# A fused four-layer network on one core: the third stage takes layer 3's mean from layer 2's integers, makes one transpose for both scales, and runs in a new order

## The chip, the cores and the metric

The kernel runs on one core of a Trainium2 chip. The metric is the device time of one launch in microseconds (us), as a median over runs. A core has five engines with queues of their own: TensorE (PE in the profile; its weight loads are PEld), VectorE (DVE), ScalarE (ACT), GpSimd (POOL) and SyncE (SP, which here only issues DMAs).

## What is computed

The input `x` has 8192 samples of 8 channels by 16 by 16, in float32. Four layers follow one another; each adds to `x` a function of its group-normalized self.

```python
def _gn(v, G=4, eps=1e-5):            # mean and variance of each sample over 2 channels x 16 x 16
    ...
    return ((g - m) / jnp.sqrt(s + eps)).reshape(v.shape)

x = x + _L0_conv_ref(_gn(x), core0, core1, core2, bias)   # a tensor-train operator
x = x + _L1_conv_ref(_gn(x), lin_w, lin_b, gamma, beta)   # 3x3 convolution, batch norm over all samples, relu
x = x + _L2_conv_ref(_gn(x), w2, b2)                      # 3x3 convolution of integers, see below
x = x + _L3_conv_ref(_gn(x), w3, b3)                      # 3x3 convolution with signs as weights, edge padding
```

Layer 2 quantizes: `sx = 127 / max|x|` over the whole normalized input of all samples, `qx = clip(round(x * sx), -127, 127)`, the weights likewise with `sw`, then an integer convolution divided by `sx * sw`, plus a bias for each channel. Layer 3 uses the signs of its weights times one mean for each output channel, pads by repeating the edge, and adds a bias.

## The kernel before, in words

The samples are cut into `NT = 64` tiles of 128 samples. A tile is `[128 partitions = 8 channels x 16 rows, 2048 = 128 samples x 16 columns]`, 1 MB. There are three stages over all 64 tiles, because the batch norm of layer 1 and the maximum of layer 2 need all samples.

*Stage 1* (to about 2620 us) does layers 0 and 1; its constants are made in `late_constants`, step by step between its tiles. *Stage 2* (to about 3063 us) applies the batch norm, takes the group means and deviations of layer 2's input (`stats2`, `sigma2`, kept for every tile in `gnst`), subtracts the mean (`centre2`), and takes the maximum of the absolute value per sample (`range2`); every fourth tile `range2` multiplies four tiles' maxima `top` by the reciprocal deviations `gr` and reduces them to one column of `amax`. Between the stages stand a reduction of `amax` to `pm`, an all-reduce over partitions to `gm`, and `sx` and `inv = 1/(sx*sw)`.

*Stage 3* (from about 3066 us) does layers 2 and 3. For each tile `i`:

- `rows2` (VectorE) multiplies one group scale by a mask into a diagonal (`diag_d`) and transposes it (`rows_d`); `spread2` (TensorE) multiplies that by `sel0`, so that `r2`, in the PSUM bank `ps_a`, holds the scale for every channel row and sample. `v` scales `x` to int8 (VectorE), `q` casts to bf16 (ScalarE), `bias` adds layer 2's bias to the first half of `x` (ScalarE).
- `c2h0` and `c2h1` (TensorE) are layer 2's convolution for the two halves of the samples, six bf16 matmuls each into the PSUM tile `pq`. `stz` (VectorE) adds the first half to `x`. For the second half `z1` (ScalarE) copies `pq` out with scale and bias and `add1` (GpSimd) adds it.
- `sq` squares the new `x` (ScalarE). `sums` (`sums_pe`, TensorE) sums `x` and its square over the rows of a group: for each of the two sources, four float32 matmuls with 32 output columns, one for each quarter of the samples, into the PSUM tile `s`. `small` (`stats_small`, VectorE) reduces `s` over the 16 columns, transposes the result into `ps_a` and makes mean and variance, `pow` (GpSimd) the reciprocal deviation.
- `rows3` makes a second diagonal of three parts (`diag_e`: mean times reciprocal deviation, reciprocal deviation, layer 2's mean) and transposes it; `spread3` makes `r3` (bank `ps_r`) and `o3` (bank `ps_o`). `c` copies `o3` with layer 3's bias (ScalarE).
- `t` scales `x` by `r3` (VectorE); `hi` and `lo` split it into two fp32r parts (ScalarE, GpSimd), `edl` and the end of `hi` copy the edges (ScalarE); `corr` adds `c` to `x` (GpSimd). `c3h0a`, `c3h0b`, `c3h1a`, `c3h1b` (TensorE) are layer 3's convolution: the letter says high or low part, the digit the half; six matmuls each into the PSUM tile `pf`, which shares two buffers of two banks with `pq`. `out0` and `out1` (VectorE) add the halves to `x`, and the tile is stored.

The order of stage 3 on every engine is written out by hand: operation `op` of tile `i` is due at `PERIOD * i + PHASE[op]`, and `todo` is the sorted list of these. The due times order the instructions only; each engine then runs its own list in this order and waits by semaphore for what it needs. `InOrder` fixes that order, and since it records every operation in its own line, nearly all instructions show as L43. The tiles `u`, `xs`, `ys`, `bs`, `xk` in profile rows are the slots in which `x` lives.

Of the kernel before, what the change touches and what calls it, by code (L numbers as in the profile page):

```python
# [8 lines left out]
F32 = mybir.dt.float32  # L9
# [4 lines left out]
ALU = mybir.AluOpType  # L14
# [18 lines left out]
class InOrder:  # L33
# [5 lines left out]
    def __getattr__(self, name):  # L39
        op = getattr(self.engine, name)  # L40

        def call(*args, **kwargs):
# [5 lines left out]
PERIOD = 11.539  # L48
PHASE = {"rows2": 0, "spread2": 0.01, "v": 5.1, "q": 10.2, "bias": 10.4, "c2h1": 11.6, "z1": 13.1, "c2h0": 16.1, "add1": 17.1,
         "stz": 23.1, "sq": 24, "sums": 31.8, "small": 34.7, "pow": 37.3, "rows3": 42.7, "spread3": 45.3, "t": 46.3,  # L50
         "hi": 49.9, "c": 51.2, "lo": 51.9, "corr": 58.8, "edl": 60.3, "c3h0a": 60.4, "c3h0b": 61.3, "out0": 66.8,
         "c3h1a": 69.3, "c3h1b": 69.4, "out1": 69.41}

# [4 lines left out]
PACK2 = [("w2all", C * C * 9), ("w3all", C * C * 9)]  # L58
# [3 lines left out]
def tile_net(ctx: ExitStack, tc: tile.TileContext, xb, xt_in, pack0, pack1, pack2, out):  # L62
# [35 lines left out]
    LATE = 5 if NT >= KEEP + STAY + 3 else 0  # L98

# [47 lines left out]
    def late_constants(late):  # L147
# [37 lines left out]
        L["grp"] = grp = blocks(32, 1.0 / 512, "grp")  # L185
        b1 = L["b1"] = const.tile([P, 1], F32, name="b1")
# [65 lines left out]
        dve.tensor_copy(gpad[:, :, 0:G], quarter.unsqueeze(1).to_broadcast([P, NQ, G]))  # L252
        for k, name in enumerate(("sel0", "sel1", "corr")):

            t = L[name] = const.tile([P, CH], F32, name=name)
            dve.tensor_copy(t.rearrange("p (g n) -> p g n", g=G),
                            mod32[:, G * k:G * k + G].unsqueeze(2).to_broadcast([P, G, CH // G]))
# [12 lines left out]
    amax = const.tile([P, NT // 4], F32, name="amax")  # L270
# [4 lines left out]
    def samples(t):  # L275
        return t.rearrange("p (b w) -> p b w", w=W)
# [425 lines left out]
    def stats_small(mv, st, ps, name):  # L702

        s = small.tile([P, 32], F32, name=f"s_{name}", tag="s")
        dve.tensor_reduce(s, samples(ps), AX.X, ALU.add)
        dve.transpose(st, s)
        sq = small.tile([P, G], F32, name=f"sq_{name}", tag="sqm")
        dve.tensor_copy(mv[:, 0:G], st[:, 0:G])
        dve.tensor_tensor(sq, st[:, 0:G], mv[:, 0:G], ALU.mult)
        dve.scalar_tensor_tensor(mv[:, G:2 * G], st[:, G:2 * G], EPS, sq, ALU.add, ALU.subtract)  # L710

# [20 lines left out]
    with tc.tile_pool(name="p2", bufs=2) as p2, tc.tile_pool(name="ps2", bufs=2, space=PSUM) as ps2:  # L732
# [16 lines left out]

        def sum2(i):  # L750
            x, y = T[i]["x"], T[i].pop("y")
            y_used[i] = y
            act.activation(y, y, AF.Relu, bias=bn_b, scale=bn_a)
            pool.tensor_tensor(x, x, y, ALU.add)
# [9 lines left out]
        def stats2(i):  # L764

            st, mv = psc[:, 32 + 32 * (i % 2):64 + 32 * (i % 2)], gnst[:, order2[i]]
            red = small.tile([P, 32], F32, name=f"s_c{i}", tag="s")
            dve.tensor_reduce(red, samples(T[i].pop("ps")), AX.X, ALU.add)
            dve.transpose(st, red)
            T[i]["sq"] = small.tile([P, G], F32, name=f"sq_c{i}", tag="sqm")  # L770
            act.copy(mv[:, 0:G], st[:, 0:G])
            act.activation(T[i]["sq"], st[:, 0:G], AF.Square)

        def sigma2(i):
            st, mv = psc[:, 32 + 32 * (i % 2):64 + 32 * (i % 2)], gnst[:, order2[i]]
            dve.scalar_tensor_tensor(mv[:, G:2 * G], st[:, G:2 * G], EPS, T[i].pop("sq"), ALU.add, ALU.subtract)
            stats_pow(mv)

        def spread2(i):
            T[i]["gb"] = ps = ps2.tile([P, BANK], F32, name=f"gb_{i}", tag="gb")  # L780
            rows = to_rows(diag[i % 2], mask2, [gnst[:, order2[i]]], f"c{i}")
            if i % 4 == 0:
                T[i]["gr"] = ps2.tile([P, 4, P], F32, name=f"gr_{i}", tag="gr")
                T[i]["top"] = p2.tile([P, 4, P], F32, name=f"top_{i}", tag="top")
            else:
                T[i]["gr"], T[i]["top"] = T[i - 1]["gr"], T[i - 1]["top"]
            for dst, sel in ((ps[:, 0:P], L["sel0"]), (T[i]["gr"][:, i % 4], L["sel1"])):
                pe.matmul(dst, sel, rows, start=True, stop=True)
# [16 lines left out]
        def range2(i):  # L805

            top = T[i]["top"]
            for a, b in HALVES:
                dve.tensor_reduce(top[:, i % 4, a:b], samples(T[i]["x"])[:, a:b], AX.X, ALU.max,
                                  apply_absolute_value=True)  # L810
            if i % 4 == 3:
                dve.tensor_tensor(top, top, T[i]["gr"], ALU.mult)
                dve.tensor_reduce(amax[:, i // 4:i // 4 + 1], top.rearrange("p a b -> p (a b)"), AX.X, ALU.max)

        def on(i, f):
            if 0 <= i < NT:
                f(i)
# [10 lines left out]
        for i in range(NT + 4):  # L828
            if i == 1:
                on(free, load2)  # L830
            if i + AHEAD2 < NT - LATE:
                on(i + AHEAD2, lambda i: i <= free or load2(i))
            elif late:
                k, j = late.pop(0)
                T2[j][k] = y_used[i - 1]
                nc.sync.dma_start(T2[j][k], (x1_d if k == "x" else y_d)[order2[j]])
            on(i, sum2)
            on(i - 2, sums2)
            on(i - 3, spread2)
            on(i - 1, square2)  # L840
            on(i - 2, stats2)
            on(i - 3, centre2)
            on(i - 2, sigma2)
            on(i - 3, range2)
# [4 lines left out]
    gm = const.tile([P, 1], F32, name="gm")  # L849
    nc.vector.tensor_reduce(pm, amax, AX.X, ALU.max)  # L850
# [3 lines left out]
    nc.vector.tensor_tensor(inv, sx, L["sw"], ALU.mult)  # L854
    nc.vector.reciprocal(inv, inv)

    gv = gnst[:, :, G:2 * G]
    nc.vector.tensor_scalar(gv, gv, sx, None, ALU.mult)
# [4 lines left out]
    with ExitStack() as s:  # L863
        wk = s.enter_context(tc.tile_pool(name="wk3", bufs=2))
        ps_c = s.enter_context(tc.tile_pool(name="ps_c3", bufs=2, space=PSUM))
        ps_s = s.enter_context(tc.tile_pool(name="ps_s3", bufs=1, space=PSUM))
        order = [*kept, *(t for t in range(NT) if t not in kept)]

        sq3, t3, z3 = sqs[0], [sqs[1], xh], [y_stay[3][:, h * F // 2:(h + 1) * F // 2] for h in range(2)]
        T = [dict() for _ in range(NT)]  # L870
        AHEAD = min(NT, KEEP - 6)
        diag2, diag3 = diagonal("d"), diagonal("e")
# [4 lines left out]
        mask, st3 = ps_a[:, P:P + NQ], ps_a[:, P + 32:P + 64]  # L877
# [12 lines left out]
        def rows2(i):  # L890
            T[i]["rows2"] = to_rows(diag2[i % 2], mask, [gnst[:, order[i], G:2 * G]], f"d{i}")

        def rows3(i):
            mv = T[i].pop("mv")
            mr = small.tile([P, G], F32, name=f"mr_{i}", tag="mr")
            dve.tensor_tensor(mr, st3[:, 0:G], mv[:, G:2 * G], ALU.mult)
            T[i]["rows3"] = to_rows(diag3[i % 2], mask, [mr, mv[:, G:2 * G], gnst[:, order[i], 0:G]], f"e{i}")


        def spread2(i):  # L900
            pe.matmul(r2, L["sel0"], T[i].pop("rows2"), start=True, stop=True)

        def spread3(i):
            rows = T[i].pop("rows3")
            pe.matmul(r3, L["sel1"], rows, start=True, stop=True)
            pe.matmul(o3, L["corr"], rows, start=True, stop=True)
# [14 lines left out]
        def bias2(i):  # L921
            x = halves(T[i]["x"])[:, 0]
            act.activation(x, x, AF.Identity, bias=L["bias2"], scale=1.0)
# [13 lines left out]

        def second2(i):
            act.activation(z3[i % 2], T[i].pop(("pq", 1)), AF.Identity, bias=L["bias2"], scale=inv)

        def add2(i):
            x = halves(T[i]["x"])[:, 1]
            pool.tensor_tensor(x, x, z3[i % 2], ALU.add)
# [4 lines left out]
        def sums3(i):  # L948
            T[i]["ps"] = ps_s.tile([P, BANK], F32, name=f"s3_{i}", tag="s3")
            sums_pe(T[i]["ps"], T[i]["x"], sq3)  # L950

        def stats3(i):
            T[i]["mv"] = small.tile([P, 2 * G], F32, name=f"mv3_{i}", tag="mv")
            stats_small(T[i]["mv"], st3, T[i].pop("ps"), f"d{i}")

        def pow3(i):
            stats_pow(T[i]["mv"])
# [44 lines left out]
        def finish(i, h):  # L1002
# [4 lines left out]
            if T[i]["done"] == 2:  # L1007
# [3 lines left out]
        OPS = {"rows2": rows2, "spread2": spread2, "v": scale2, "q": round2, "bias": bias2,  # L1011
               "c2h0": lambda i: layer2(i, 0), "stz": first2, "c2h1": lambda i: layer2(i, 1), "z1": second2, "add1": add2,
               "sq": square3, "sums": sums3, "small": stats3, "pow": pow3, "rows3": rows3, "spread3": spread3, "c": offset3,
# [3 lines left out]
        todo = [(op, i) for _, op, i in sorted((PERIOD * i + at, op, i) for op, at in PHASE.items() for i in range(NT))]  # L1017
        for i in range(AHEAD):
            load3(i)
        for op, i in todo:  # L1020
            if op == "rows2" and AHEAD <= i + 4 < NT:
                load3(i + 4)
            OPS[op](i)

# [68 lines left out]
```

## Time and profile before

| | |
|---|---|
| median of 3 runs | 3824.15 us (3823.85 to 3824.85) |
| profiled execution, own time / span | 3824.58 / 3822.8 us |
| busy over the span | PE 94%, DVE 89%, POOL 80%, ACT 66% |
| stage 1, 0 to 2620 us | PE busy 2601.65, DVE 2311.57 |
| stage 2, 2620 to 3062 us | DVE busy 395.72, DMA share 0.94 |
| stage 3, 3062 to 3823 us | PE busy 738.24, POOL 721.85, DVE 678.72, ACT 583.94 |

Busy shares are of the span, so an engine may be full in one stage and idle in another. A profile row gives a group of instructions as `out<-in`, the shape, the count, and the mean time of one in nanoseconds; durations overlap where instructions are pipelined, so that the step from one start to the next start is what an engine pays in a full queue.

### The profile page before, as it was taken

The numbers are of one execution on the slowest core, as the hardware profiler recorded it, in microseconds if no ns is written. First come the engines' busy times: TensorE is split into PE (matmuls) and PEld (weight loads), VectorE is DVE, ScalarE is ACT, GpSimd is POOL, SyncE is SP. The second block draws the span as 40 slices with busy tenths as digits, with TensorE's granted clock in tenths as the row PEclk, the third lists the DMA queues.
The fourth block names the chain that finished last, engine by engine and source line by source line (L and its number), as shares of the span: only waits on it lengthen the run. The fifth ranks groups of instructions, "written<-read, shape, count | busy, mean of one in ns | idle before, by whom it ended". The sixth has DMA issues, their size and how long they took to land.

```text
span 3822.8 us, 52777 instructions
## 1 busy us (share of the span) xinstructions
PE 3598.8 (94%) x16264; PEld 2127.1 (56%) x16326; DVE 3386.0 (89%) x6313; ACT 2518.2 (66%) x2676; POOL 3048.8 (80%) x3104
## 2 busy tenths in 40 slices
PE   8999999999999999999999999997665589999999
PEld 4666666666666666666666666663221145555555
DVE  8988888888888888888888888877998889999997
ACT  5666666666666666666666666665665578778775
POOL 4877777778777777787777777865887779999998
PEclk9999999999999999999999999998776689999999
DMA  5787787878877878878788878766999724444442
GB/s 212 254 270 256 258 269 252 265 258 258 271 253 261 272 253 262 262 250 272 254 263 270 257 258 265 253 200 253 419 424 424 326 90 186 182 183 187 181 161 110
DMA packets 210809, 960.93 MB, mean 251 GB/s; under 512 B 44896, under 2 KB 45152, under 8 KB 110048
## 3 DMA queue, kind: packets, MB, share of 16 engines
q1 hardware_dynamic: 173808, 692.22, 48.8%
q0 software_dynamic: 36288, 264.26, 23.5%
q8 instruction: 131, 2.15, 0.2%
q14 instruction: 150, 1.23, 0.1%
q10 hardware_dynamic: 432, 1.08, 0.1%
HBM read 578.84 MB, written 378.54 MB: 250 GB/s over the span
## 4 chain that ended last, share of the span: by engine, by line
PE 85%; DVE 6%; DMA 4%; issue 2%; POOL 1%; ACT 1%; POOLq 0%; SPq 0%; DVEq 0%; ACTq 0%
PE po L43 45%; PE pu L43 12%; PE pf L43 10%; PE pm L43 6%; PE pq L43 4%; PE s L43 3%; PE pc L43 3%; DVE top L43 3%; PE ps_r L43 1%; DMA ys<-x_d 1%; DMA x_d<-u 1%; DMA x_d<-ys 1%; DMA u<-x_d 1%; DMA x_d<-xs 1%; DMA sq<-y_d 1%
## 5 line engine op out<-in xcount | busy, mean ns | idle before, releaser
L43 PE MATMUL po<-u,core 128*128 128x512 f32 (+1 forms) x4112 | 1844.7, 591 | 0.0
L43 ACT COPY u<-pu 128x2048 f32<-128x2048 f32 x512 | 955.4, 1866 | 512.9 <-PE pu L43 512.8
L43 PEld LDWEIGHTS po<-u,core 128*128 128x128 f32 x4112 | 744.6, 190 | 737.0 <-issue 736.1
L43 PE MATMUL pu<-core2r,xl 128*128 128x256 f32 x4032 | 678.6, 310 | 4.5 <-ACT u L43 3.5
L43 PEld LDWEIGHTS pu<-core2r,xl 128*128 128x128 f32 x4032 | 527.9, 189 | 127.9 <-issue 123.1
L43 POOL TENSOR_TENSOR bs<-bs,xh 128x512 fp32r<-128x512 f32 (+1 forms) x253 | 325.1, 1285 | 203.0 <-ACT xh L43 203.0
L43 POOL TENSOR_TENSOR v<-e 128x128 f32<-128x128 f32 x750 | 396.7, 540 | 0.0
L43 DVE TENSOR_TENSOR xs<-po,xs 128x512 f32<-128x512 f32 x256 | 176.9, 691 | 218.8 <-PE po L43 218.6
L43 ACT ACTIVATE m<-pm,b 128x128 f32<-128x128 f32 x250 | 91.7, 367 | 395.3 <-PE pm L43 395.3
L43 PEld LDWEIGHTS pm<-v,fast 128*128 128x128 f32 x2000 | 262.5, 192 | 119.7 <-issue 105.7
L43 POOL TENSOR_TENSOR e<-x1n,x 128x512 f32<-128x512 f32 x250 | 305.9, 1223 | 23.2 <-ACT x L43 15.8
L43 DVE TENSOR_TENSOR bs<-bs,stat 128x1024 f32<-128x1024 f32 x252 | 290.6, 1215 | 2.1
L43 POOL TENSOR_TENSOR xs<-xs,w 128x2048 f32<-128x2048 f32 x64 | 291.4, 4552 | 0.6 <-DMA xs<-in_xt 0.6
L43 PE MATMUL pm<-v,fast 128*128 128x128 f32 x2000 | 263.6, 275 | 0.0
L43 ACT ACTIVATE x<-x1n 128x512 f32<-128x512 f32 x500 | 247.0, 545 | 7.6 <-DVE x1n L43 7.6
L43 POOL TENSOR_TENSOR mv<-mv,mhalf 128x4 f32<-128x4 f32 x127 | 130.8, 1030 | 135.9 <-DVE mv L43 135.9
L43 PE MATMUL pf<-hi,sign 128*128 128x512 f32 x768 | 231.1, 439 | 0.0
L43 POOL DMA_DIRECT2D xl<-limb_d x252 | 149.8, 594 | 101.3 <-ACT x L43 38.4
L43 PE MATMUL pf<-lo,sign 128*128 128x512 f32 x768 | 218.0, 422 | 0.3 <-ACT lo L43 0.3
L43 POOL TENSOR_TENSOR v<-r 128x128 f32<-128x128 f32 x500 | 215.2, 447 | 0.0
L43 ACT ACTIVATE sq<-xs 128x2048 f32<-128x2048 f32 x103 | 197.0, 1913 | 18.2 <-DVE xs L43 13.6
L43 PE MATMUL gb<-rows_c,sel 128*128 128x128 f32 x128 | 40.8, 413 | 166.3 <-DVE rows_c L43 166.3
(308 smaller groups left out, 7195.3 us busy)
## 6 DMA issues: line engine op xcount, KB each, us to landing
xl<-limb_d POOLq DMA_DIRECT2D x252, 1024.0 KB, 7.4
x_d<-xs SPq DMA_DIRECT2D x76, 1024.0 KB, 8.4
xs<-in_xt SPq DMA_DIRECT2D x64, 1024.0 KB, 7.6
bs<-in_xb SPq DMA_DIRECT2D x63, 1024.0 KB, 5.6
limb_d<-xh SPq DMA_DIRECT2D x1008, 64.0 KB, 4.4
limb_d<-bs SPq DMA_DIRECT2D x1008, 64.0 KB, 5.2
y_d<-ys SPq DMA_DIRECT2D x60, 1024.0 KB, 8.0
u<-x_d SPq DMA_DIRECT2D x34, 1024.0 KB, 6.5
```

Of the source, the lines that this page charges most:

```text
L43: return self.tc.keep_in_program_order(op(*args, **kwargs))
```

## The change

It touches three places.

In the setup the bias of layer 2 gets its group mean taken off, which moves to layer 3's bias. A small job at tile 8 of stage 2 (`operands3`) makes bf16 weights `total` that sum layer 2's convolution over output rows, and a selection matrix `back2`.

In stage 3 `sums` no longer multiplies `x`: it multiplies the integers `q` by `total` (high and low part of the weights, three column taps each, four quarters: 24 bf16 matmuls, of which eight cover 512 columns and sixteen 32). `cols` holds, for each tile, four columns of group values side by side: layer 3's two, layer 2's mean, and layer 2's scale of the tile `LEAD = 4` later. So one product, one transpose and three matmuls (`rows`, `spread`) serve both scales, and the separate `rows2` and `spread2` go. The squared mean (`sqm`) is ScalarE's, the variance (`var`) stays on VectorE. Of the second half of layer 2, `SHARE = 16` samples (256 of 1024 columns) go to VectorE (`stz1`); `bias` covers them. The table of due times is new.

At the end of stage 2 `range2` finishes tiles 60 to 62 with tile 62 and tile 63 by itself, and `inv` is made later, after the first scaling.

```diff
-PERIOD = 11.539
-PHASE = {"rows2": 0, "spread2": 0.01, "v": 5.1, "q": 10.2, "bias": 10.4, "c2h1": 11.6, "z1": 13.1, "c2h0": 16.1, "add1": 17.1,
-         "stz": 23.1, "sq": 24, "sums": 31.8, "small": 34.7, "pow": 37.3, "rows3": 42.7, "spread3": 45.3, "t": 46.3,
-         "hi": 49.9, "c": 51.2, "lo": 51.9, "corr": 58.8, "edl": 60.3, "c3h0a": 60.4, "c3h0b": 61.3, "out0": 66.8,
-         "c3h1a": 69.3, "c3h1b": 69.4, "out1": 69.41}
+PERIOD = 10.966
+PHASE = {"v": 0, "q": 3.7, "c2h1": 10.5, "bias": 10.6, "stz1": 12.1, "z1": 12.9, "c2h0": 14, "stz": 15.2, "add1": 17.2,
+         "sq": 20.8, "sums": 21.9, "small": 23.5, "sqm": 25.4, "var": 26.5, "pow": 30.4, "rows": 32.9, "spread": 33.3,
+         "c": 35, "t": 41.2, "hi": 43.2, "lo": 49, "edl": 52.9, "corr": 55.8, "c3h1a": 61.3, "c3h1b": 61.5, "c3h0a": 62.1,
+         "c3h0b": 62.4, "out1": 65, "out0": 65.8}
+LEAD = 4
+SHARE = 16
...
+        pair = w["bias2all"].rearrange("p (g k) -> p g k", k=C // G)
+        dve.tensor_tensor(pair, pair, grp.unsqueeze(2).to_broadcast([P, G, C // G]), ALU.mult)
+        mb = const.tile([P, 1], F32, name="mb")
+        dve.tensor_reduce(mb, w["bias2all"], AX.X, ALU.add)
+        dve.tensor_scalar(mb, mb, 512.0 * G / C, None, ALU.mult)
+        dve.tensor_tensor(L["bias2"], L["bias2"], mb, ALU.subtract)
+        dve.tensor_tensor(L["bias3"], L["bias3"], mb, ALU.add)
...
+        def operands3():
+            part = const.tile([P, 3, G], F32, name="part")
+            total = L["total"] = const.tile([P, 6, 32], BF16, name="total")
+            dve.memset(total, 0.0)
+            dve.tensor_reduce(part.rearrange("p k g -> p (k g)"), L["band2"].rearrange("p k (g n) -> p (k g) n", g=G), AX.X, ALU.add)
+            for k in range(0, 3, 2):
+                dve.tensor_tensor(part[:, 1], part[:, 1], part[:, k], ALU.add)
+                dve.tensor_scalar(part[:, k], part[:, k], -1.0, None, ALU.mult)
+            dve.tensor_copy(total[:, 0:3, 0:G], part)
+            dve.tensor_tensor(total[:, 3:6, 0:G], part, total[:, 0:3, 0:G], ALU.subtract)
+            L["select"]("back2", [3], L["band3"][:, 0])
...
-            if i % 4 == 3:
-                dve.tensor_tensor(top, top, T[i]["gr"], ALU.mult)
-                dve.tensor_reduce(amax[:, i // 4:i // 4 + 1], top.rearrange("p a b -> p (a b)"), AX.X, ALU.max)
+            if i % 4 == 3 or i == NT - 2:
+                a, b, at = (3, 4, i // 4) if i == NT - 1 else (0, i % 4 + 1, NT // 4 if i == NT - 2 else i // 4)
+                dve.tensor_tensor(top[:, a:b], top[:, a:b], T[i]["gr"][:, a:b], ALU.mult)
+                dve.tensor_reduce(amax[:, at:at + 1], top[:, a:b].rearrange("p a b -> p (a b)"), AX.X, ALU.max)
...
+    cols = wk.tile([P, NT + LEAD, 4 * G], F32, name="cols", bufs=1)
+    nc.vector.memset(cols[:, 0:LEAD, 0:3 * G], 0.0)
+    nc.vector.memset(cols[:, NT:, 3 * G:4 * G], 0.0)
+    nc.scalar.copy(cols[:, LEAD:, 2 * G:3 * G], gnst[:, :, 0:G])
...
-    nc.vector.tensor_tensor(inv, sx, L["sw"], ALU.mult)
-    nc.vector.reciprocal(inv, inv)
-
-    gv = gnst[:, :, G:2 * G]
-    nc.vector.tensor_scalar(gv, gv, sx, None, ALU.mult)
+    nc.vector.tensor_scalar(cols[:, 0:NT, 3 * G:4 * G], gnst[:, :, G:2 * G], sx, None, ALU.mult)
...
+        def column(i, k):
+            return cols[:, i + LEAD, k * G:(k + 1) * G]
 
         def rows3(i):
-            mv = T[i].pop("mv")
-            mr = small.tile([P, G], F32, name=f"mr_{i}", tag="mr")
-            dve.tensor_tensor(mr, st3[:, 0:G], mv[:, G:2 * G], ALU.mult)
-            T[i]["rows3"] = to_rows(diag3[i % 2], mask, [mr, mv[:, G:2 * G], gnst[:, order[i], 0:G]], f"e{i}")
+            if i >= 0:
+                dve.scalar_tensor_tensor(column(i, 0), st3[:, 0:G], inv512, column(i, 1), ALU.mult, ALU.mult)
+            diag = diag3[i % 2]
+            dve.tensor_tensor(diag[:, :, 0:4 * G], cols[:, i + LEAD].unsqueeze(1).to_broadcast([P, NQ, 4 * G]),
+                              mask.unsqueeze(2).to_broadcast([P, NQ, 4 * G]), ALU.mult)
+            T3[i] = rows = small.tile([P, P], F32, name=f"rows_{i}", tag="rows")
+            dve.transpose(rows, diag.rearrange("p q j -> p (q j)"))
 
         def spread3(i):
-            rows = T[i].pop("rows3")
-            pe.matmul(r3, L["sel1"], rows, start=True, stop=True)
-            pe.matmul(o3, L["corr"], rows, start=True, stop=True)
+            rows = T3.pop(i)
+            for k, (dst, sel) in enumerate(((r2, "back2"), (r3, "sel1"), (o3, "corr"))):
+                if (i >= 0 if k else i + LEAD < NT):
+                    pe.matmul(dst, L[sel], rows, start=True, stop=True)
...
         def bias2(i):
-            x = halves(T[i]["x"])[:, 0]
+            x = T[i]["x"][:, 0:F // 2 + SHARE * W]
...
+        def third2(i):
+            x = halves(T[i]["x"])[:, 1][:, 0:SHARE * W]
+            dve.scalar_tensor_tensor(x, T[i]["pq", 1][:, 0:SHARE * W], inv, x, ALU.mult, ALU.add)
+
         def second2(i):
-            act.activation(z3[i % 2], T[i].pop(("pq", 1)), AF.Identity, bias=L["bias2"], scale=inv)
+            act.activation(z3[i % 2][:, SHARE * W:], T[i].pop(("pq", 1))[:, SHARE * W:], AF.Identity, bias=L["bias2"], scale=inv)
 
         def add2(i):
-            x = halves(T[i]["x"])[:, 1]
-            pool.tensor_tensor(x, x, z3[i % 2], ALU.add)
+            x = halves(T[i]["x"])[:, 1][:, SHARE * W:]
+            pool.tensor_tensor(x, x, z3[i % 2][:, SHARE * W:], ALU.add)
...
         def sums3(i):
             T[i]["ps"] = ps_s.tile([P, BANK], F32, name=f"s3_{i}", tag="s3")
-            sums_pe(T[i]["ps"], T[i]["x"], sq3)
+            ps, qs = T[i]["ps"], samples(T[i]["q"])
+            for j in range(2):
+                for k, w in ((1, slice(0, W)), (0, slice(W - 1, W)), (2, slice(0, 1))):
+                    for q in range(NQ):
+                        pe.matmul(samples(ps)[32 * q:32 * q + 32, :, w], L["total"][:, 3 * j + k],
+                                  qs[:, q * QS:(q + 1) * QS, w], start=(j == 0 and k == 1), stop=False)
+            for q in range(NQ):
+                pe.matmul(ps[32 * q:32 * q + 32], L["wsum"][:, 1], sq3[:, q * BANK:(q + 1) * BANK], start=False, stop=True)
 
         def stats3(i):
-            T[i]["mv"] = small.tile([P, 2 * G], F32, name=f"mv3_{i}", tag="mv")
-            stats_small(T[i]["mv"], st3, T[i].pop("ps"), f"d{i}")
+            red = small.tile([P, 32], F32, name=f"s_{i}", tag="s")
+            dve.tensor_reduce(red, samples(T[i].pop("ps")), AX.X, ALU.add)
+            dve.transpose(st3, red)
+
+        def square_mean3(i):
+            T[i]["sqm"] = small.tile([P, G], F32, name=f"sqm_{i}", tag="sqm")
+            act.activation(T[i]["sqm"], st3[:, 0:G], AF.Square, scale=inv512)
+
+        def variance3(i):
+            dve.scalar_tensor_tensor(column(i, 1), st3[:, G:2 * G], EPS, T[i].pop("sqm"), ALU.add, ALU.subtract)
...
         for op, i in todo:
-            if op == "rows2" and AHEAD <= i + 4 < NT:
+            if not ready and op not in ("rows", "spread", "v"):
+                ready = True
+                dve.tensor_tensor(inv, sx, L["sw"], ALU.mult)
+                dve.reciprocal(inv, inv)
+                dve.tensor_scalar(inv512, inv, 1.0 / 512, None, ALU.mult)
+            if op == "v" and AHEAD <= i + 4 < NT:
                 load3(i + 4)
             OPS[op](i)
...
```

## The prediction

> **What bounds it now.** Start with the page's chain of waits, then ask which stage the change is in.
>
> ```profile
> PE 85%; DVE 6%; DMA 4%; issue 2%; POOL 1%; ACT 1%; POOLq 0%; SPq 0%; DVEq 0%; ACTq 0%
> ```
>
> TensorE carries most of the chain. The change lies mainly in the third stage (3066 to 3818 us), so read busy time by stretches of ten tiles there (after the span: PE, PEld, DVE, ACT, POOL, clock, DMA share, GB/s):
>
> ```profile
> 3223.00:3337.70 114.70, 114.17 (x571) 67.52 (x580) 105.43 (x191) 91.32 (x81) 113.64 (x41) 1.00 0.49 186
> 3337.70:3452.40 114.70, 114.18 (x572) 67.52 (x580) 105.43 (x191) 91.29 (x81) 112.81 (x41) 1.00 0.47 181
> ```
>
> Both PE and POOL look full, which busy time alone can't settle. The chain inside one tile does:
>
> ```profile
> 3231.30 1.85 PE s L43 x16
> 3233.15 0.42 PE ps_r L43 x2
> 3233.57 0.22 PE ps_o L43 x2
> 3233.79 0.22 PE ps_a L43 x2
> 3234.02 1.30 PE pq L43 x6
> 3235.31 6.15 PE pf L43 x24
> 3241.46 0.66 PE pq L43 x3
> 3242.12 0.05 issue
> 3242.18 0.59 PE pq L43 x2
> 3242.77 1.85 PE s L43 x16
> ```
>
> These pieces sum to the 11.47 us from one `s` to the next; no other engine appears. So the tile period is TensorE's own sum, 11.47, and POOL stands just below: per tile lo 4.28, corr 3.69, add1 2.42, pow 1.02 = 11.41 by the groups. A microsecond taken off POOL, DVE or ACT is worth nothing alone; one off `s` is worth 64.
>
> Inside `s`, TensorE's timeline for one tile:
>
> ```profile
> 3426.27 1.07 PE L43 MATMUL s<-bs,wsum 128*32 128x512 f32 x8
> 3427.16 1.04 PE L43 MATMUL s<-sq,wsum 128*32 128x512 f32 x8
> 3428.13 0.49 PE L43 MATMUL ps_r<-rows_e,sel 128*128 128x128 f32 x2
> ```
>
> Start to start, the x half takes 0.89 and the square half 0.97. Single records explain it: four matmuls, one for each group of 32 output columns, start 7 ns apart and run together, in two fp32 passes 0.43 apart.
>
> **What the skill says.** "TensorE: Matmul & The Clock Gate", Part 3, says that matmuls on different column groups run concurrently: the 7 ns agree. Its "Wait — 56ns, not 53.3ns?" gives a floor of 25 ns between matmuls however small, and 62 ns each where the sequencer decodes them in software: no small bf16 matmul runs in this trace, so these become upper prices below. "PSUM — Partial Sum Buffer", "PSUM bank collisions raise a hardware error", has ScalarE and VectorE kept off one bank even as two readers. The trace agrees: late in stage 2 VectorE subtracts one half of `gb` and needs nothing from ScalarE, yet waits for ScalarE's copy `gm` of the other half of that bank. From the waits (total, times, longest, us):
>
> ```profile
> DVE yk L43 <- ACT gm L43: 0.8, 2, 0.4
> ```
>
> **Part 1: the mean from layer 2's integers.** Removed: the x half, 0.88 (single records). Added: for each of two bf16 weight parts, a full 512-column set of four concurrent matmuls and two edge sets of 32 columns: 24 matmuls, 24 weight loads. A full bf16 set of 512 columns is paced at 0.216 (pq's pace), so two cost 0.43. Four edge sets: lower bound 4 × 0.02 (28 ns of starts at 7 ns); upper, four starts at the skill's 25 ns, 0.10 each. I take 0.045, since each weight load must precede its matmuls and cannot hide behind so short a set. With 0.03 for the first load: 0.43 + 0.18 + 0.03 = **0.64**, between 0.52 and 0.88. The switch to column groups (pq's last start to `s` is 0.31 instead of 0.216) stays. Gain 0.24 per tile, 15.6 us over 64; bounds 0 and 23. The layer-2 integers are read later, so ScalarE's q of two tiles on must wait for them (two buffers). Behind q on ScalarE stand edl and sq; but q also waits for v, which ends later than those sums do, so this wait should not bind.
>
> **Part 2: one diagonal and transpose.** VectorE loses diag_d 0.16, rows_d 0.31, two of three diag_e 0.33, the mv copy 0.16 and sq_d 0.16: 1.12 busy. The remaining diagonal grows to 64 elements, +0.05; the product mr becomes one instruction of like cost. ScalarE gains the squared mean, about 0.18 (stage 2's sq_c row). PE still runs three spread matmuls a tile. var now waits for that squared mean, with t and out1 behind it on VectorE; stz stands between small and var, 1.2 us in which ScalarE has 0.2 us to do. v's scale now comes from the spread of the tile four before, so v waits for nothing new: VectorE's order is v, rows, and only then can PE overwrite r2. Worth nothing by itself: PE covers it.
>
> **Part 3: a quarter of the second half moves.** 256 of 1024 columns leave add1 (2.42 → 1.81 POOL), go to VectorE (1242 ns for 1024 scales to about 0.44), and make bias 1.15 → 1.36 and z1 1.19 → 0.98 on ScalarE. POOL's sum becomes 10.81. This matters: had POOL stayed at 11.41, it would have kept nearly all of part 1.
>
> **Part 4: the new order.** A fixed order on four engines runs at its longest loop: an engine's own sum, or a chain that returns to its start one period later. Take both. TensorE: 11.47 - 0.24 = **11.23**. POOL 10.81. VectorE, start to start: before 11.47 - 0.62 idle (waiting on pf) = 10.85; less about 0.75 and plus 0.36 (issue-spaced), 10.5. ScalarE about 9.7 (hi and its edges 2.45, sq 1.91, q 1.90, bias 1.36, z1 0.98, edl 0.55, c 0.36, squared mean 0.2). The new wait is z1 behind stz1 (same bank). Its loop: layer-2 half 0 ends, 0.2, stz 1.17, var 0.15, t 2.29, out1 1.19, v 2.26, rows 0.68, out0 1.16, stz1 0.51, z1 1.03, matmul start 0.1 = 10.75. z1 releases the bank pair for layer 3's first half; behind it on ScalarE stand c, squared mean and q. 10.75 < 11.23, so TensorE stays the bound with POOL 0.4 behind; whatever the sums cost, no more can be had than 11.47 → 10.8.
>
> **Part 5: from the last range to the first scaling.** On VectorE now:
>
> ```profile
> 3055.84 0.18 DVE L43 TENSOR_TENSOR diag_b<-gnst,mask 128x32 f32<-128x32 f32 x1
> ...
> 3059.59 2.34 DVE L43 TENSOR_REDUCE top<-sq 128x64 f32<-128x1024 f32 x2
> 3059.70 0.32 SPq L803 DMA_DIRECT2D x_d<-sq  x1
> 3062.03 0.69 DVE L43 TENSOR_TENSOR top<-top,gr 128x512 f32<-128x512 f32 x1
> 3062.76 0.69 DVE L43 TENSOR_REDUCE amax<-top 128x1 f32<-128x512 f32 x1
> ```
>
> The last pair shrinks from 512 to 128 elements: about -0.8. But tile 62's new pair over 384 (2 × 0.6) comes ahead of tile 63's diagonal in VectorE's program order, hence on the same path: +1.2. inv and its reciprocal leave: -0.1 to -0.2; two small memsets and a wider diagonal, +0.2. Net +0.4 (-0.8 to +0.8): this way isn't shorter. inv's three instructions run while v(1) waits for its spread (idle 0.89). The cols copy is ScalarE's, idle there.
>
> **Rest.** Tile 8 of stage 2 gets some ten small VectorE instructions, about 1.7 us, where VectorE is on the chain; later the DMA engines, full from 2700 to 3000, carry it and can absorb part: +0.8 (0 to 1.7). Setup instructions in stage 1: +0.2 (0 to 1), PE's 2602 of 2620 us covering them. The pack grows by 32 bytes a partition: nothing. No DMA issue is added; load3 moves from rows2 to v, SP alone, and 13 slots keep loads tiles ahead. Four early spreads: +0.3 at the stage's start. Filling and draining: the first five periods weren't PE-bound (v starts 3.7 to 8.4 apart), so the gain counts about 60 times rather than 64 (+1.0), which layer 3's two halves, now one period apart no more, may give back: -1.0; ±3.
>
> Sum: -15.6 + 0.4 + 0.8 + 0.2 + 0.3 = **-13.9**. Profiled execution 3824.58 (span 3822.8): 3810.7. It stood 0.43 above the median 3824.15, so the median goes to **3810.2**.
>
> **Rivals.** *A, no gain:* edge sets at the skill's 25 ns a start make the new sums 0.88: period 11.47 and only the +1.7 of the other terms remains: 3826. For: 24 weight loads behind tiny matmuls, with strided reads and writes; against: 7 ns starts. *B, slower:* TensorE's sequencer can't feed 48 short instructions. At 62 ns a matmul the sums take 1.49, +0.61 a tile or 39 us: 3865. It decides from 37 ns a matmul (0.88/24). Against: in stage 1, right behind a wait for `xh`, four loads and four matmuls start within 27 ns, so they had been decoded during the wait; and a period has about 150 PE and PEld records in 11.2 us, 75 ns each, which stage 1 reaches (79 over 20 us). *C, slower:* the z1/stz1 loop exceeds 11.47; it has 0.7 to go. *D, floor:* edge sets nearly free and a shorter drain: a period of 11.1, 23 us and 3 more, about 3800. *E, part 5 doesn't do what it says:* worked out above as +0.4; its whole price either way is under 1 us, so it has no case of its own.
>
> **Numbers.** A measurement tells 0.2%, 7.6 us, from no change. Mine 0.70, D 0.10: faster 0.80. A 0.09. B 0.08 and C 0.03: slower 0.11. Range 3795 (edge sets free, fill and drain 3 better, stage 2 free, and 2 of unlisted spread) to 3826 (A's end), leaving out B, C and the rest.
>
> **What would show it.** Per tile: `s<-q` from first start to the first `s<-sq` start near 0.64; period near 11.23; PE still alone in the chain; POOL idle about 0.4; VectorE idle 0.7; z1 waits on stz1 or not, PE not idle behind it; v(0) no earlier against the last `top`. Wrong if PE idles each tile, or if the sums take over 0.88.

## The result, and the profile after

The changed kernel takes 3817.88 us (median of 20 runs, 3815.72 to 3821.19) against 3823.92 for the kernel before beside it (20 runs): a ratio of 0.9984, 95% interval 0.9977 to 0.9991. That is 6.0 us less, 0.16%: a real gain, since the interval leaves out 1, but less than half of the 13.9 forecast, and short of the 7.6 us that the prediction called the least a measurement can tell. The profiled executions differ by 7.2 us (3824.58 to 3817.41, spans 3822.8 to 3815.6), and only these two can be taken apart.

First, where it stands now. The chain of waits by engine, from the page after:

```profile
PE 86%; DVE 6%; DMA 5%; issue 1%; POOL 1%; ACT 1%; SPq 0%; DVEq 0%; POOLq 0%; ACTq 0%
```

Then ten tiles twice in the third stage (length, then busy time of PE, PEld, DVE, ACT, POOL, TensorE's clock, DMA share, GB/s):

```profile
3223.00:3336.30 113.30, 112.78 (x732) 69.19 (x741) 101.14 (x141) 91.82 (x91) 107.45 (x41) 1.00 0.49 186
3336.30:3449.60 113.30, 112.78 (x731) 69.18 (x741) 101.15 (x141) 91.78 (x91) 107.20 (x41) 1.00 0.48 186
```

Only TensorE is full now. POOL has come down from 113.6 of 114.7 to 107 of 113.3. The chain inside one tile (start, length, what) is still TensorE alone:

```profile
3399.75 0.42 PE ps_a L43 x2
3400.17 0.22 PE ps_r L43 x2
3400.39 0.22 PE ps_o L43 x2
3400.61 0.65 PE pq L43 x3
3401.26 0.05 issue
3401.31 0.60 PE pq L43 x2
3401.91 6.21 PE pf L43 x24
3408.12 1.31 PE pq L43 x6
3409.43 1.65 PE s L43 x29
```

So the kind of bound is as forecast. The period, the mean step from one `v` to the next over tiles 15 to 55, went from 11.473 to **11.327**, not to 11.23. The chain rounds the ends of instructions; sizes are better read from starts. TensorE's timeline of one tile, before and then after (start, length, shapes, count):

```profile
3407.06 1.90 PE L43 MATMUL pf<-hi,sign 128*128 128x512 f32 x6
...
3413.40 1.47 PE L43 MATMUL pq<-q,band 128*128 128x512 bf16 x5
3414.80 1.07 PE L43 MATMUL s<-ys,wsum 128*32 128x512 f32 x8
3415.68 1.04 PE L43 MATMUL s<-sq,wsum 128*32 128x512 f32 x8
```

```profile
3401.56 1.91 PE L43 MATMUL pf<-hi,sign 128*128 128x512 f32 x6
...
3407.96 1.47 PE L43 MATMUL pq<-q,band 128*128 128x512 bf16 x6
3409.36 0.85 PE L43 MATMUL s<-q,total 128*32 128x512 bf16 x24
3410.03 1.05 PE L43 MATMUL s<-sq,wsum 128*32 128x512 f32 x8
```

From `s<-ys` to `s<-sq` it was 0.88; from `s<-q` it is 0.67. But from the first `pf` to the next `pq` it was 6.34, and is now 6.40: layer 3's 24 matmuls, which the change does not touch, became slower. The same pieces as means over some 38 tiles, in us:

| TensorE, start to start | before | after |
|---|---|---|
| mean of layer 3 (`s<-x` or `s<-q`) | 0.883 | 0.666 |
| squares (`s<-sq`) | 0.972 | 0.979 |
| three spreads | 0.772 | 0.772 |
| layer 2 before and after (`pq`, two pieces) | 2.510 | 2.510 |
| layer 3 (`pf`) | **6.338** | **6.400** |
| sum | 11.474 | 11.327 |

The 7.2 us between the profiled executions are therefore: from the start to `v` of tile 0, 2.6 less; from there to the last layer-3 matmul, 749.4 to 744.7, 4.7 less; the end, 0.1 more. Over 64 tiles the period alone would give 9.4, so filling and draining took 4.7 back. Three things need a cause: 6.40, the fill, and the 2.6 us ahead of the third stage.

At the boundary VectorE now does this:

```profile
3052.91 0.55 DVE L43 TENSOR_TENSOR top<-top,gr 128x384 f32<-128x384 f32 x1
3053.50 0.55 DVE L43 TENSOR_REDUCE amax<-top 128x1 f32<-128x384 f32 x1
3053.97 0.18 DVE L43 TENSOR_TENSOR diag_b<-gnst,mask 128x32 f32<-128x32 f32 x1
...
3060.16 0.29 DVE L43 TENSOR_TENSOR top<-top,gr 128x128 f32<-128x128 f32 x1
3060.48 0.28 DVE L43 TENSOR_REDUCE amax<-top 128x1 f32<-128x128 f32 x1
```

The pair over 384 stands ahead of tile 63's diagonal and costs 1.2 there; behind the last range the way to `v` of tile 0 is 0.7 shorter (4.58 to 3.88). From tile 50's range to that `v` it was 91.9 and is 91.9.

### The profile page after: what moved, and what is told of

Its sections match the earlier page's. It is cut to its first block, busy times and chain, and to the rows that moved or that the text cites. A ratio compares the mean times of both kernels' runs of the same rounds, so it can differ in the third digit from the quotient of the medians.

```text
span 3815.6 us, 54624 instructions
## 1 busy us (share of the span) xinstructions
PE 3590.2 (94%) x17286; PEld 2137.8 (56%) x17350; DVE 3364.9 (88%) x6020; ACT 2524.9 (66%) x2741; POOL 3015.9 (79%) x3102
## 4 chain that ended last, share of the span: by engine, by line
PE 86%; DVE 6%; DMA 5%; issue 1%; POOL 1%; ACT 1%; SPq 0%; DVEq 0%; POOLq 0%; ACTq 0%
PE po L43 45%; PE pu L43 12%; PE pf L43 10%; PE pm L43 6%; PE pq L43 4%; PE pc L43 3%; PE s L43 3%; DVE top L43 2%; DMA u<-x_d 1%; DMA sq<-y_d 1%; PE ps_a L43 1%; DMA ys<-x_d 1%; DMA x_d<-u 1%; DMA x_d<-ys 1%; DMA x_d<-xs 1%
## 5 line engine op out<-in xcount | busy, mean ns | idle before, releaser
L43 ACT ACTIVATE m<-pm,b 128x128 f32<-128x128 f32 x250 | 91.9, 368 | 396.0 <-PE pm L43 396.0
L43 PE MATMUL pq<-q,band 128*128 128x480 bf16 (+1 forms) x704 | 188.3, 387 | 10.1 <-ACT q L43 6.4
```

The source lines that it names most:

```text
L43: return self.tc.keep_in_program_order(op(*args, **kwargs))
```

## Experiments: why layer 3's matmuls became slower

The change had moved nearly every buffer: the third stage's by 3616 bytes, and all large ones from 32 past a multiple of 64 onto one. **Alignment** was the first theory, the swapped order of layer 3's halves its rival. The first kernel adds 32 bytes to the changed one, the second the same to the kernel before:

```diff
     pool.memset(mhalf, -0.5)
+    pad = const.tile([P, 8], F32, name="pad")
+    pool.memset(pad, 0.0)
```

> The changed kernel with 32 bytes more in the constants, so that every large buffer starts at 32 past a multiple of 64 as in the kernel before, not on it. Theory 1 (alignment): layer 3's 24 matmuls go back from 6.40 to 6.34 us a tile, the period from 11.327 to 11.26, 64 tiles give 4 us: about 3813.8. It may also undo the 3 us that stage 2 gained in its DMA-bound stretch, which would then leave about 3817. Rival (order of the halves, or other engines' accesses): 6.40, period 11.327, about 3818.

> The kernel before with the same 32 bytes more, so that its large buffers start on multiples of 64. Theory 1: layer 3's matmuls go from 6.34 to 6.40 us a tile, the period from 11.473 to about 11.54, about 3828, less 3 if the alignment also helps stage 2's transfers. Rival: 6.34, 11.473, about 3824.

Measured: e1 keeps 6.402 us for `pf` (period 11.337; 3819.05 us, ratio 0.9988, 0.9980 to 0.9997), e2 keeps 6.338 (period 11.473; 3821.77, ratio 0.9994, 0.9986 to 1.0002). So it doesn't matter to `pf` whether all buffers together lie on a multiple of 64 or 32 past it. The same shift does account for most of the 2.6 us, below. The third kernel swaps the halves' due times:

```diff
-"c3h1a": 61.3, "c3h1b": 61.5, "c3h0a": 62.1, "c3h0b": 62.4, "out1": 65, "out0": 65.8
+"c3h0a": 61.3, "c3h0b": 61.5, "c3h1a": 62.1, "c3h1b": 62.4, "out0": 65, "out1": 65.8
```

> The changed kernel with layer 3's first half ahead of its second in the order, nothing else. Theory 2 (the order of the halves makes layer 3's matmuls slower): 6.34 us a tile, period 11.26, about 3814. Theory 1 (alignment): 6.40, 11.327, about 3818.

Measured: 6.400, period 11.327, 3817.86 us (ratio 0.9984, 0.9978 to 0.9991). The order isn't it either. Both theories had fallen. What the 32 bytes had *not* changed is the **distance** between layer 3's weights and its moving operand, `hi` and `lo`: 163808 bytes before and in e2, 167360 after and in e1. The next two kernels change it by moving `hi` and `lo`, and with them `q` and what else lies behind the gap: the changed kernel gets 544 bytes ahead of the third stage's tiles (distance 163808 + 4096), the kernel before 3552 (exactly 167360).

```diff
     wk = ctx.enter_context(tc.tile_pool(name="wk3", bufs=2))
+    pad = wk.tile([P, 136], F32, name="pad", bufs=1)      # in the kernel before: [P, 888]
+    pool.memset(pad, 0.0)
```

> The changed kernel with 544 bytes ahead of the third stage's tiles, so that the distance from layer 3's weights to its moving operand is that of the kernel before plus 4096. Theory 3 (weights and moving operand disturb each other by their distance in SBUF): layer 3's matmuls go from 6.40 to 6.34 us a tile, period 11.26. Theory 4 (it comes with the new instruction stream, not with an address): 6.40, 11.327.

> The kernel before with 3552 bytes ahead of the third stage's tiles, so that the distance from layer 3's weights to its moving operand is exactly that of the changed kernel. Theory 3: layer 3's matmuls go from 6.34 to 6.40 us a tile, period 11.536, about 3827. Theory 4: 6.34, 11.473, about 3823.5.

Measured: in e5 `pf` takes 6.333 and the period is 11.262. In e6 it takes 6.368, and the timeline shows that the tiles, which take turns in two sets of buffers, differ by turns, 6.38 and 6.35:

```profile
3400.65 1.90 PE L43 MATMUL pf<-hi,sign 128*128 128x512 f32 x6
...
3407.03 1.47 PE L43 MATMUL pq<-q,band 128*128 128x512 bf16 x5
...
3412.17 1.91 PE L43 MATMUL pf<-hi,sign 128*128 128x512 f32 x6
...
3418.52 1.47 PE L43 MATMUL pq<-q,band 128*128 128x512 bf16 x5
```

So the place of the third stage's tiles matters: 544 bytes further on, the changed kernel has its fast layer 3 back, and the new distance alone gives half of the 0.06 to the kernel before. The other half comes only together with the new sums (e7 below, the new place with the old sums, has 6.368 as well). What it is about the place isn't separated. The weights hardly moved, so that distance and place are one here; the distances of the fast kernels, 163808 and 167904, agree modulo 4096, but already modulo 64 both differ from 167360; and `q` moved along. Which access meets which isn't shown either. The Trainium skill ("SBUF — State Buffer", "SBUF: two separate sides") says that among the engines only the port pair shared by VectorE and GpSimd causes contention; these runs show a matmul stream that is 1% slower for the place of its tiles all the same, without showing that it waits for another engine.

The times of e5 and e6, 3820.08 (0.9991, 0.9982 to 0.9999) and 3831.14 (1.002, 1.0012 to 1.0028), hold a cost of the experiment itself. POOL's timeline in e5:

```profile
3062.71 0.21 POOL L43 MEMSET pad<- 128x136 f32 x1 [8.81 <-DVE amax L43]
3068.59 0.38 POOL L885 PARTITION_ALL_REDUCE gm<-pm  x1 [5.67 <-issue]
```

The clearing of the gap waited for the last range, and POOL then took 5.67 us to begin the all-reduce; in the changed kernel the all-reduce starts at 3061.23, 0.5 after the last `amax`. The Trainium skill ("GPSIMD Engine Reference", "2.1 Instruction dispatch") puts about 6 us on the first call of a freshly loaded kernel, and the 5.67 fits. Without the clearing, POOL is idle for 9 us ahead of the all-reduce; that such a load is hidden there is likely, but not shown. In e6 the all-reduce starts 5.3 later than in the kernel before, and layer 3's 0.03 over 64 tiles is 1.9: together 7.2 of the 7.3 us by which its median is above that kernel's. So e10 takes the gap inside the tile `cols`, with nothing on POOL:

```diff
-    cols = wk.tile([P, NT + LEAD, 4 * G], F32, name="cols", bufs=1)
+    cols = wk.tile([P, (NT + LEAD) * 4 * G + 136], F32, name="cols", bufs=1)
+    cols = cols[:, 0:(NT + LEAD) * 4 * G].rearrange("p (i k) -> p i k", k=4 * G)
```

> The changed kernel with layer 3's moving operand 544 bytes further on, the gap taken inside the tile ahead of it, so that nothing new stands on POOL ahead of the maximum over partitions. Theory 3: layer 3's matmuls 6.33 us a tile, period 11.26, the way from the last maximum to gm back at 0.5 us, so 4 us less than the changed kernel: about 3814. If the 6 us ahead of gm comes from the place and not from the memset on POOL: about 3820.

Measured: `pf` 6.335, period 11.264, `gm` 0.5 after `amax`, span 3811.3. TensorE's timeline of one tile:

```profile
3410.59 1.89 PE L43 MATMUL pf<-hi,sign 128*128 128x512 f32 x6
...
3416.91 1.47 PE L43 MATMUL pq<-q,band 128*128 128x512 bf16 x6
3418.32 0.86 PE L43 MATMUL s<-q,total 128*32 128x512 bf16 x24
```

Here `pf` takes 6.32. Two tiles on it takes 6.40 again:

```profile
3433.10 1.90 PE L43 MATMUL pf<-hi,sign 128*128 128x512 f32 x6
...
3439.50 1.47 PE L43 MATMUL pq<-q,band 128*128 128x512 bf16 x6
```

In the steady part of e5 and e10 every ninth tile does so and all others take 6.32 to 6.33; nine is odd, so both sets of buffers have slow tiles and fast ones. The place, then, isn't all that decides: what else does is open.

The profiled execution is 4.3 us under the changed kernel's span, as expected (3813.2 by its own time). The median is not: 3816.95 (0.9982, 0.9975 to 0.9990). The single runs fall into seven from 3812.7 to 3815.1, with the profiled one among them, and nine from 3816.5 to 3820.5. What the slower ones do isn't seen, since a trace shows one execution; that stays open, and with it how much of the 4 us the new place saves on the whole.

**What the 32 bytes did do.** Time from the first range of stage 2 to tile 8's, 40's and 50's, in us:

| | tile 8 | tile 40 | tile 50 |
|---|---|---|---|
| kernel before, 32 past 64 | 50.8 | 253.3 | 328.4 |
| e6, 32 past 64 | 50.6 | 253.4 | 328.0 |
| e2: before, on 64 | 50.8 | 253.5 | 326.1 |
| changed kernel, on 64 | 55.1 | 257.7 | 326.0 |
| e1: changed, 32 past 64 | 55.2 | 257.7 | 328.1 |

The other kernels with their large buffers on 64 lie between 325.8 and 327.0 at tile 50. Between tiles 40 and 50 the DMA engines carry the stage, and two things happen there. Buffers on multiples of 64 rather than 32 past them save some 2 us, which nobody had planned. (Some of them, those named `yk`, then start on multiples of 256 as well, so which multiple counts isn't separated.) And the 4.4 us by which the changed kernel is late since tile 8 vanish whole.

Those 4.3 to 4.4 us are `operands3`, forecast at 1.7. VectorE's timeline at tile 8, and POOL's beside it:

```profile
2673.54 0.49 DVE L43 TENSOR_REDUCE part<-band 128x12 f32<-128x384 bf16 x1
2674.07 2.79 DVE L43 TENSOR_TENSOR part<-part 128x4 f32<-128x4 f32 x1
2676.89 0.17 DVE L43 TENSOR_SCALAR part<-part 128x4 f32<-128x4 f32 x1
2676.97 0.15 DVE L43 TENSOR_TENSOR part<-part 128x4 f32<-128x4 f32 x1
```

```profile
2672.34 4.50 POOL L43 TENSOR_TENSOR xk<-xk,yk 128x2048 f32<-128x2048 f32 x1
```

Adding four columns to four takes 2.79, its twin 0.15. The long one ends with POOL's addition, at 2676.84. That fits the port pair of the section named above, which says that a VectorE instruction with two SBUF inputs and a GpSimd one that reads SBUF exclude each other for a whole instruction. No run here moves the addition away from POOL's, so the cause is read from the trace, not tested.

## Experiments: what bounds the period

e4 leaves out layer 3's mean (the mean counts as 0), so that TensorE has 0.67 us less to do:

```diff
-            for j in range(2):
-                for k, w in ((1, slice(0, W)), (0, slice(W - 1, W)), (2, slice(0, 1))):
...
-                pe.matmul(ps[32 * q:32 * q + 32], L["wsum"][:, 1], sq3[:, q * BANK:(q + 1) * BANK], start=False, stop=True)
+                pe.matmul(ps[32 * q:32 * q + 32], L["wsum"][:, 1], sq3[:, q * BANK:(q + 1) * BANK], start=True, stop=True)
```

> The changed kernel without the 24 matmuls of layer 3's mean (the mean is left out, the squares stay). If TensorE's own sum alone sets the period, it falls by the whole 0.666 us to 10.66, and the time by 43 us to about 3775. If the loop over z1 and stz1 or POOL stands where the prediction put it, the period stops at 10.8 and PE shows some 0.14 us of idle time a tile, about 3784.

Measured: 3780.42 us (0.9887, 0.9872 to 0.9903), period 10.70. The largest and the fourth of the waits of TensorE's weight loads (total, times, longest):

```profile
PEld ps_a L43 <- DVE rows L43: 34.4, 41, 0.8
PEld pf L43 <- ACT bs L43: 11.0, 41, 0.4
```

The first was there in the changed kernel too, 0.8 a tile, on other instructions of VectorE. The second is new: layer 3's first weight load waits for `z1` (which writes the slot `bs`), and the start of `pf` comes 1.23 after `pq`, where it was 1.11. So TensorE is held up by others in every tile. Ten tiles show by whom it can be (columns as above; PE's figure counts modelled ends, which cover its waits):

```profile
3327.00:3434.00 107.00, 107.00 (x501) 64.05 (x500) 101.07 (x141) 92.05 (x91) 107.00 (x41) 1.00 0.52 196
```

POOL is busy all of the time and waits for nothing in these tiles, while ScalarE's squares wait for its addition. From start to start POOL's four instructions take 10.69. So POOL's own sum, 10.81 in the prediction, is the likeliest bound at 10.70. The loop over `stz1` and `z1`, worked out at 10.75, shows its waits as well (`z1` some 0.9 a tile for `stz1`) and can't be far, but no run separates the two. Of the 0.67 us all but 0.04 come back, but not as plainly as that looks: with the pauses `pf` itself took 6.30 in the mean, from 6.24 to 6.38, with its operands where the changed kernel has them.

e7 undoes part 1 alone: it brings the float32 sums over `x` back into the changed kernel (`inv512` becomes 1, since these sums come out as means):

```diff
+            sums_pe(T[i]["ps"], T[i]["x"], sq3)
...
-                dve.tensor_scalar(inv512, inv, 1.0 / 512, None, ALU.mult)
+                dve.tensor_scalar(inv512, inv, 0.0, 1.0, ALU.mult, ALU.add)
```

> Part 1 alone undone: the changed kernel with layer 3's mean again from the fp32 matmuls over x. By TensorE's own sum the x half goes from 0.666 to 0.87 or 0.88 us, and the period to 11.53 to 11.54, so about 13 us more, 3831: slower than the kernel before, whose layer 3 matmuls take 6.34. If layer 3's extra 0.06 comes with the new sums, the period is 11.47 and the time about 3827.

Measured: 3827.18 us (1.0009, 1.0000 to 1.0018), period 11.503, the x half 0.883, `pf` 6.368. The period is 0.177 above the changed kernel's, 0.217 from the sums less 0.032 and 0.008 that layer 3 and the squares give back. Against the changed kernel's median the integers' mean is worth 9.3 us, and without it the change is no gain: all other parts together cost some 3 us against the kernel before (0 to 7 by the interval).

e8 undoes part 3 alone (`stz1` then does nothing):

```diff
-SHARE = 16
+SHARE = 0
```

> Part 3 alone undone: the quarter of the second half goes back to ScalarE and POOL (no stz1). By POOL's own sum (10.45 busy in the changed kernel, plus 0.6 and its gaps) the period is 11.41 to 11.45 with POOL as the bound, 5 to 8 us more than the changed kernel, 3823 to 3826. If POOL isn't near the bound: 11.327 and 3818.

Measured: 3817.42 us (0.9983, 0.9976 to 0.9990), period 11.333. Ten tiles of it:

```profile
3220.00:3333.30 113.30, 112.78 (x732) 69.10 (x741) 98.10 (x131) 92.75 (x90) 112.90 (x41) 1.00 0.49 186
```

POOL is busy for 11.29 of 11.33 us and still doesn't bind. Part 3 is worth nothing here, less than a hundredth of a us a tile. With layer 3 at its old 6.34 TensorE's sum would be 11.26, below 11.29, and it would matter by a few hundredths.

## Experiments: the fill and the boundary

In the fill, after `v` of tile 0, TensorE's pauses of over 0.3 us sum to 7.9 before and to 12.5 after, in the drain to 0.6 and 0 (4.0 of the 4.7 together), and layer 3's first matmul comes 32.2 us after that `v` before and 43.2 after. Its place in the drain shows in the chain of the end: 72 matmuls of layer 3, three tiles, with nothing between them.

```profile
3790.41 18.64 PE pf L43 x72
```

TensorE's work had been pushed out of the fill. The longest pauses of the fill wait for `q`, such as this of 2.00 us (the bracket gives the pause and what ended it):

```profile
3081.32 1.95 PE L43 MATMUL pq<-q,band 128*128 128x512 bf16 x6 [2.00 <-ACT q L43]
```

Two kernels try to shorten it by another order of the first tiles alone. In both, the table `FIRST` replaces due times for tiles 0 to 5 (e12: 0 to 4):

```diff
+FIRST = {"c2h0": 10.7, "stz": 12.3}                                            # e9
+FIRST = {"rows": 32.3, "hi": 43.6, "corr": 48.1, "lo": 55.2, "edl": 56.9}      # e12
```

> The changed kernel with another order for tiles 0 to 5 of the third stage alone: layer 2's half 0 stands right behind half 1 on TensorE, ahead of the sums and spreads of the tile before, and stz right behind stz1 on VectorE. Theory 5 (the longer fill comes from half 0 standing behind the sums of the tile before, so that each early tile waits for the squares of the last): TensorE's idle time in the fill goes from 12.5 us back to about 8 as in the kernel before, the time by some 4 us to 3814. Rival (ScalarE's and POOL's order makes the fill long): idle 12 or more, about 3818.

Measured: 3822.02 us (0.9996, 0.9988 to 1.0004). The pauses grew to 15.7, three of them waits of `pq` for `q` of 2.4 to 3.2. The theory falls: with layer 2 moved up, the sums come later, and behind them the squared mean, which stands ahead of `q` on ScalarE. Two lines of ScalarE's timeline in e9 show it:

```profile
3098.90 0.26 ACT L43 ACTIVATE sqm<-ps_a,inv 128x4 f32<-128x4 f32 x1 [0.71 <-DVE ps_a L43]
3099.06 1.89 ACT L43 CAST q<-v 128x2048 bf16<-128x2048 int8 x1
```

> The kernel of e10 with another order for tiles 0 to 4 of the third stage alone: POOL's corr stands ahead of lo, lo behind the add1 of the tile three on, hi behind that tile's bias on ScalarE, rows ahead of v on VectorE. Theory 6 (POOL's lo of 4.3 us ahead of add1, with the squares and layer 2 of later tiles behind it, makes the fill long): layer 3's first matmul comes 3 to 4 us sooner after the first v than e10's 43.3, TensorE's idle time in the fill falls from 12.5 to about 8, and the time by 3 to 5 us against e10's 3817, to about 3813. Rival (the fill is set by each tile's own chain of operations, whatever the order): idle 12 or more, about 3817.

Measured: 3815.83 us (0.9984, 0.9977 to 0.9990); the first layer-3 matmul after 43.1 us instead of e10's 43.3, the pauses 15.2 instead of 12.6, and from `v` of tile 0 to the last layer-3 matmul 741.2 us in both. The steps from one early `v` to the next were only dealt out anew. This theory falls too, and it shows that the sum of pauses is a rough measure: 2.6 us more of them cost nothing. So the pauses place the 4 us in the fill, ahead of layer 3's first matmul, but what in the new order makes them is open.

e11 has the edits of e9 and e10, and puts the pair over tiles 60 to 62 behind tile 63's diagonal and transpose:

```diff
+            if i - 3 == NT - 1:
+                pair2(NT - 2)
```

> Three edits together: the place of e10, the order of e9 in the fill, and in stage 2 the maximum over tiles 60 to 62 put behind tile 63's diagonal and transpose, where VectorE waits for tile 63's spread. The last costs 0 where it now costs 1.1. If all three add up: 4 + 4 + 1, about 3809. If the fill's order does nothing: about 3813.

Measured: 3819.00 us (0.9988, 0.9980 to 0.9996), which carries e9's longer fill (pauses 15.7). Its boundary:

```profile
3054.45 0.31 DVE L43 STREAM_TRANSPOSE rows_c<-diag_b 128x128 f32<-128x128 f32 x1
3056.14 0.55 DVE L43 TENSOR_TENSOR top<-top,gr 128x384 f32<-128x384 f32 x1 [1.38 <-PE gr L43]
3056.72 0.55 DVE L43 TENSOR_REDUCE amax<-top 128x1 f32<-128x384 f32 x1
```

The pair didn't fill the wait for tile 63's spread; it waited 1.38 us for that spread's `gr`, which TensorE writes into the bank from which the pair reads, and stood ahead of the subtraction all the same. From tile 62's range to `v` of tile 0 it is 13.6, no better than in the changed kernel (13.5; 12.9 before). An instruction put into a gap must not depend on what ends the gap. Of these kernels, the lowest medians (e12 3815.83, e10 3816.95, e8 3817.42) can't be told from the changed kernel's 3817.88.

## Why the prediction was right or wrong, step by step

- **The bound: right.** TensorE was the bound and stayed it; POOL's idle time came to 0.6 (0.4 forecast), `z1` does wait for `stz1` in every tile (some 1.0 us), and TensorE doesn't pause behind it.
- **Part 1: right in kind, 0.03 short.** The mean takes 0.666 where 0.64 stood. The edge sets cost about what was forecast: single records give each 0.04 to 0.06 from its start to the next set's, 0.20 for the four, with the four matmuls of a set 3 to 4 ns apart, as "TensorE: Matmul & The Clock Gate" of the Trainium skill has it ("Measured speedup vs the span model"). The two full sets took 0.46 rather than 0.43. Gain 13.9 instead of 15.6 us; the squares gave 0.5 back. Rival B's price can be checked too: the new sums took 28 ns a matmul, under the 37 from which it would have decided.
- **The step that failed: "Part 4: TensorE 11.47 - 0.24 = 11.23".** It assumed that the rest of the sum stays as it was. Layer 3's matmuls took 0.0625 more, 4.0 us over 64 tiles, and the period came to 11.327. That the change moved the third stage's tiles brings this about: e5 and e10 undo it by place alone, e6 brings half of it by place alone. What about the place does it is open.
- **Filling and draining, 0 ± 3: mis-sized.** 4.7 us, past its range. That layer 3's halves "may give back" 1.0 was wrong: the drain was already nearly free of pauses.
- **Part 2, part 3, part 4's loops.** Part 2 was forecast to be worth nothing by itself; no run undoes it alone. That POOL at its old sum "would have kept nearly all of part 1" was wrong: the 11.41 added instruction lengths, which overlap; e8 shows 11.29 at work. That no more can be had than 10.8 was right to 0.1 (10.70 in e4), with POOL's sum the likeliest bound there; that the loop of 10.75 binds isn't shown.
- **Part 5: right.** Not shorter: +1.2 and -0.7, as worked out; from tile 62's range to `v` +0.5 (forecast +0.4), and from tile 50's no change.
- **The rest.** `operands3` took 4.4 of VectorE instead of 1.7 and cost nothing at the end (forecast +0.8): the DMA-bound stretch absorbed all of it. No term stood for the 2 us that the 64-byte starts gave that stretch. Small slips in the sums change nothing: 0.24 times 64 is 15.4 rather than 15.6, the loop's terms add up to 10.74, rival A's sums to 0.86 rather than 0.88, and the 75 ns that stage 1 was said to reach are 79 there.

In us, in place of the forecast -13.9 in all, the profiled executions show: -13.9 (mean) + 0.5 (squares) + 4.0 (place of layer 3's operands) + 4.7 (fill and drain) - 2.6 (stage 2) + 0.1 = -7.2. Rivals A to D didn't come: the period lies where neither free nor dear edge sets would have put it, and the time came out midway between the forecast and A for two reasons that were none of the rivals. That it lies well inside the range is in part luck, since the 2.6 us of stage 2 made up for some of the 8.7 lost to the other two; and 0.80 for a gain of over 7.6 us was too much.

## What to carry to other kernels

A change that adds or drops a constant can move every buffer behind it, and where a stage runs at one engine's pace for 64 tiles a hundredth of that pace is several us: compare the pieces that you did *not* change, from start to start, before believing a sum. A gain for each tile has to be counted from where the stage becomes bound by that engine; a new order is paid in the fill. Before putting a small job beside a busy POOL, or a small instruction on an idle one, look at what that engine does at that moment.

## What the runs showed of the hardware that was not expected

- Layer 3's 24 float32 matmuls take 6.33 or 6.40 us in the mean depending on where the third stage's tiles lie (e5, e10; changed kernel), 6.34 and 6.37 in the kernel before and e6. In e5 and e10 every ninth tile takes 6.40 all the same.
- Stage 2's DMA-bound stretch ends about 2 us sooner with the large buffers on multiples of 64 bytes than 32 past them (326.1 and 328.4 at tile 50 in e2 and the kernel before, 326.0 and 328.1 in the changed kernel and e1).
- A 128x4 addition on VectorE took 2.79 us instead of 0.15, ending with POOL's 4.50 us addition (changed kernel).
- POOL's all-reduce began 5.67 us after a memset put right ahead of it (e5; 5.63 in e6), and 0.5 us after the last `amax` where POOL had been idle (changed kernel, e10).
